# Layer-0 block attention: queries and outputs by seven block products, softmax sums on ScalarE, one PSUM bank for each kind of result

## The chip, the cores and the metric

The kernel runs on one core of a Trainium2 chip. The metric is the device time of one launch in microseconds (us); for one core that is the time of the core itself. A time is the median of several runs. Everything is computed in fp32.

The engines are named as in the profile: PE is TensorE (matmuls and transposes), PEld its weight loads, DVE is VectorE, ACT is ScalarE, POOL is GpSimd, SP is SyncE, which issues most DMAs. A matmul takes a stationary operand (its "weights", here mostly 128x128) and streams a moving operand of up to 512 columns through it. An fp32 matmul shows as two records in the trace. Results land in PSUM, which has eight banks of 128 x 512 fp32.

## The reference, cut to what matters

A decoder of two layers over x of shape (8, 112, 512), which is 896 tokens. Each layer has self-attention, cross-attention to a context, and a feed-forward part. The feed-forward part of layer 0 is itself a block: attention with 32 query heads and 4 key/value heads of dimension 128, and then a mixture of 32 experts. The change is in that inner attention:

```python
h = _rmsnorm(hidden_states, ln1_w)             # (8, 112, 512)
q = (h @ Wq).reshape(B, S, 32, 128)            # Wq: 512 x 4096
k = (h @ Wk).reshape(B, S, 4, 128)
v = (h @ Wv).reshape(B, S, 4, 128)
q = _rope(q, pos); k = _rope(k, pos)
k = jnp.repeat(k, 8, axis=2); v = jnp.repeat(v, 8, axis=2)
scores = jnp.einsum('bqhd,bkhd->bhqk', q, k) / sqrt(128)
scores = jnp.where(causal, scores, -1e9)
attn = softmax(scores)
o = jnp.einsum('bhqk,bkhd->bqhd', attn, v).reshape(B, S, 4096) @ Wo   # Wo: 4096 x 512
x = resid + o
...
h = _rmsnorm(x, ln2_w)                         # then the router and the experts
```

## The kernel before, in words

Tokens are held in seven tiles of 128 (`x[t]`, `y[t]`), and the normalised tokens transposed as `hT`, four 128-row chunks (`KC`) of 896 columns, used in two halves of 448 (`HALF`). `y` is the residual and the sum of the block.

`l0_block_attention` first computes keys `kT`, values `v` and the queries of the first head group. Then it runs over eight head groups `hg` of four heads each, and in a group over the eight sequences `b` of 112 tokens. A head group reads one 512x512 slice of Wq (`wq`) and one of Wo (`wo`). A step (hg, b) issues:

- `probabilities`: four score matmuls (L888) into a `sc_ps` bank, then on DVE scale and mask (L893), row maximum (L898) and its subtraction (L297), on ACT one exp for four heads (L298), on DVE the sum (L901) and reciprocal (L903), on POOL the product by it (L904).
- `gather_weights`: the expert weights are copied into one DRAM tensor for the experts stage, 192 copies of 256 KB spread over the 64 steps (L931). A tiny DMA that reads a row of `s` (L929) makes these copies keep pace with the attention, since SP issues its queue in order.
- `project_queries`: one of eight query blocks of the next head group, four matmuls of 448 columns (L259), and its rope (`rope_halves`): one DVE product (L841), two half products (L844), one POOL addition (L848).
- `average` of the step two before: four transposes of the probabilities (L304), an ACT copy `pT` (L306), the product with the values (L913), an ACT copy into `oT` (L917).
- `project_out` of a token tile some five steps before (`LAG`): four matmuls of 512 columns (L259) and a DVE addition into `y` (L922).

Matmul banks (0, 1), score banks (2, 3), transpose banks (4, 5) and output banks (6, 7) go in turns of two. In this block the order on each engine is left to the tile scheduler, before and after the change: the Python order is a priority, and the scheduler moves instructions of an engine against one another. Buffers come from pools with a set number of slots, and a new tile in a slot waits for the last reader of the old one.

Layer 1's feed-forward already forms its matmuls as block products by `seven_products` (in the listing after the change it has moved up). It splits both operands in 2x2 blocks. Eight block products become seven, on sums of blocks: `row_sums` makes four sums of the stationary blocks and `column_sums` four of the moving blocks. The seven products go to banks a, b and c, where some add up in place, and some are copied by ACT (L1414) so that they can be added to more than one result. Its sums and combinations are L1387 to L1397 and L1961 to L1972, its last additions into `x` L2021.

Of the kernel before, what the change touches and what calls it, by code (L numbers as in the profile page):

```python
# [58 lines left out]
def decoder(ctx: ExitStack, tc: tile.TileContext, a, out: bass.AP):  # L59
# [756 lines left out]

    def block_norm(y, t, root):

        mvr = row_scales(x[t], root, (ONCE, twice(1e-5)))
        yield  # L820
        xn = normed_rows()
        normed(xn, x[t], mvr, mvr[:, 3:4])
        shift = sm.tile([P, 1], FP, tag="shift", name="shift", bufs=8)
        V.tensor_scalar(shift, mvr[:, 0:1], mvr[:, 2:3], -1.0, ALU.mult, ALU.mult)
        A.activation(y[t], x[t], AF.Identity, bias=shift, scale=mvr[:, 2:3])
        return xn
# [23 lines left out]
    def l0_block_attention(y, hT, late, weights, prepare):  # L850
# [5 lines left out]

        wk_, wv = load_w(a["f0_wk"], "f0_wk"), load_w(a["f0_wv"], "f0_wv")
        with phase("f0", "tile") as p0:
            kT = p0.tile([P, 4, NT], FP, tag="kT", name="kT")
# [10 lines left out]
            v = p0.tile([S, B, D], FP, tag="v", name="v")  # L870
            for half in range(2):
                for g in range(4):
                    rope_halves(kT[:, g, half * HALF : (half + 1) * HALF], project_T(hT, wk_, g, half))
                for j in range(4):
                    project_queries(qT, wq, 4 * half + j)
                if half == 0:
                    for xn, t in late:
                        transpose_tile(hT, xn, t, ln1w)
            for b in range(B):
                pp = mm_ps()  # L880
                matmul_k(pp[:S, :], lambda k: hT[:, k, b * S : (b + 1) * S], lambda k: wv[:, k, :])
                A.copy(v[:, b, :], pp[:S, :])

            def probabilities(hg, qT, b):
                sc = sc_ps()
                tok = slice(b * S, (b + 1) * S)
                for j in range(4):
                    T.matmul(  # L888
                        sc[:S, j * S : (j + 1) * S], qT[:, j, tok], kT[:, hg // 2, tok],
                        start=True, stop=True,  # L890
                    )
                s = work[0].tile([S, 4, S], FP, tag="s", name="s", bufs=4)
                V.scalar_tensor_tensor(  # L893
                    s, sc[:S, : 4 * S].rearrange("p (j q) -> p j q", j=4),
                    128.0**-0.5, causal4, ALU.mult, ALU.add,
                )
                mx = sm.tile([S, 4], FP, tag="mx", name="mx")
                V.tensor_reduce(mx, s, AX.X, ALU.max)  # L898
                softmax_exp(s, mx)
                den = sm.tile([S, 4], FP, tag="den", name="den")  # L900
                V.tensor_reduce(den, s, AX.X, ALU.add)  # L901
                rec = sm.tile([S, 4], FP, tag="rec", name="rec")
                V.reciprocal(rec, den)  # L903
                G.tensor_tensor(s, s, rec.unsqueeze(2).to_broadcast([S, 4, S]), ALU.mult)  # L904
                return s

            outs = o_ps()

            def average(hg, oT, b, s):
                pT = transpose_probs(s, "pT")  # L910
                po = outs[b % 2]
                kv = hg // 2
                T.matmul(  # L913
                    po[:, : 4 * S], v[:, b, kv * P : (kv + 1) * P],
                    pT.rearrange("p j q -> p (j q)"), start=True, stop=True,
                )
                A.copy(  # L917
                    oT[:, :, b * S : (b + 1) * S], po[:, : 4 * S].rearrange("p (j q) -> p j q", j=4)
                )

            def project_out(oT, wo, t):
                V.tensor_tensor(y[t], y[t], project_rows(oT, wo, t), ALU.add)  # L922

            halves = [a[n].rearrange("e p k n -> (e p) (k n)") for n in ("e0_wg", "e0_wu", "e0_wd")]

            def gather_weights(step, s):
# [3 lines left out]
                for i, src in enumerate(halves):  # L930
                    nc.sync.dma_start(weights[r, i * KC * NI : (i + 1) * KC * NI], src[r, :])  # L931

            waiting, finished = [], []
            for hg in range(8):
# [4 lines left out]
                else:  # L939
                    prepare()  # L940
                for b in range(B):
                    waiting.append((hg, oT, b, probabilities(hg, qT, b)))
                    gather_weights(hg * B + b, waiting[-1][3])
                    if hg < 7:
                        project_queries(qT_next, wq, b)
                    if len(waiting) > 2:
                        average(*waiting.pop(0))

                    if b < NTT:
                        finished.append((oT, wo, b))  # L950
                    if len(finished) > LAG:
                        project_out(*finished.pop(0))
                qT = qT_next
            for one in waiting:
                average(*one)
            for one in finished:
                project_out(*one)
# [424 lines left out]


    def row_sums(dst, top, bottom, eng):


        eng.tensor_tensor(dst(0), bottom[0], bottom[1], ALU.add)  # L1387
        eng.tensor_tensor(dst(1), dst(0), top[0], ALU.subtract)
        eng.tensor_tensor(dst(2), top[0], bottom[0], ALU.subtract)
        eng.tensor_tensor(dst(3), top[1], dst(1), ALU.subtract)  # L1390

    def column_sums(dst, left, right, eng):

        eng.tensor_tensor(dst(0), right[0], left[0], ALU.subtract)  # L1394
        eng.tensor_tensor(dst(1), right[1], dst(0), ALU.subtract)
        eng.tensor_tensor(dst(2), right[1], right[0], ALU.subtract)
        eng.tensor_tensor(dst(3), left[1], dst(1), ALU.subtract)  # L1397

    def seven_products(banks, n, terms, top, bottom, rows, left, right, columns, copies, take):

        a, b, c = (bank[:, :n] for bank in banks)

        def product(dst, lhs, rhs, first=False, part=None):
            for k in range(terms) if part is None else part:
                T.matmul(dst, lhs(k), rhs(k), start=first and k == 0, stop=k == terms - 1,  # L1410
                         skip_group_check=True)

        def copied(i):
            A.copy(copies[i], a)  # L1414
            return copies[i]

        few = range(terms if terms < 4 else terms // 2)
        product(a, top[0], left[0], first=True)
        m1 = copied(0)
        yield  # L1420
        product(c, rows[0], columns[0], first=True)
        product(a, rows[1], columns[1])
        u2 = copied(1)
        product(b, top[1], left[1], first=True, part=few)
        product(a, rows[2], columns[2])
        u3 = copied(2)
        yield
        take(1, 1, c, u3)
        product(b, top[1], left[1], part=range(len(few), terms))
        take(0, 0, b, m1)  # L1430
        product(a, bottom[1], columns[3])
        take(1, 0, a, None)
        product(c, rows[3], right[1])
        take(0, 1, c, u2)

    def in_turn(products):

        last = iter(())
        for one in products:
            next(one)  # L1440
            all_of(last)
            next(one)
            last = one
        all_of(last)
# [471 lines left out]
    def l1_feed_forward():  # L1916


        with phase("f1") as p0:
# [4 lines left out]
            def of_hT(k, half):  # L1924
                return lambda kk: hT[:, 2 * k + kk, half * HALF : (half + 1) * HALF]

            def of(block):
                return lambda kk: block[:, kk, :]

            with ExitStack() as pools:  # L1930
                gp = pools.enter_context(tc.tile_pool(name="gates", bufs=1))
                tokens = [gp.tile([P, 2, HALF], FP, tag=f"tok{i}", name=f"tok{i}") for i in range(4)]
                for kk in range(2):
                    column_sums(lambda i: tokens[i][:, kk, :],
                                *([of_hT(k, half)(kk) for k in range(2)] for half in range(2)), V)

                def projected(w, p, banks, take):

                    def block(m, k):
                        c = (2 * p + m) * P  # L1940
                        return w[:, 2 * k : 2 * k + 2, c : c + P]

                    sums = gp.tile([P, 4, 2, P], FP, tag="sums", name="sums", bufs=3)
                    row_sums(lambda i: sums[:, i], *([block(m, k) for k in range(2)] for m in range(2)),
                             G)
# [3 lines left out]
                        banks, HALF, 2, *([of(block(m, k)) for k in range(2)] for m in range(2)),  # L1949
                        [of(sums[:, i]) for i in range(4)],  # L1950
                        *([of_hT(k, half) for k in range(2)] for half in range(2)),
                        [of(t) for t in tokens], copies, take,
# [196 lines left out]
```

## Time and profile before

| | |
|---|---|
| median of 3 runs | 2036.39 us (2034.69 to 2037.57) |
| the profiled execution | 2040.25 us |
| its span, first to last instruction | 2038.4 us |
| mean granted TensorE clock | 0.976 of full speed |
| PE busy | 1930.7 us, 95% of the span |
| DVE, ACT, POOL busy | 956.7, 589.5, 723.2 us |
| DMA | 209.65 MB, 103 GB/s on average |

The profile is one execution. Busy times are shares of the whole span, an average over stages with different limits, so the stage that is changed is read by itself: in the stretch from 406.7 to 897.8 us the attention loop runs. Lines with a line number (L259) belong to the source line, and where a helper such as `matmul_k` issues the work of several callers, they are told apart by the names of the operands. `f_wq` is a query weight slice, `f_wo` an output one. A group's row reads: line, engine, operation, output<-inputs, shapes, count, then busy us and the mean duration in ns, then the idle time of the engine before it and what ended it. A row of the timeline reads: start, length, engine, line, operation, and how many records are put together in it. A row of a tile has the shortest, median and longest duration in ns and the first and last start.

### The profile page before, as it was taken

To read this page: it belongs to the slowest core of one execution; us is meant where nothing else is said; L and a number is where in the kernel's file an instruction comes from. 1 tells how busy PE (TensorE), PEld (TensorE's weight loads), DVE (VectorE), ACT (ScalarE), POOL (GpSimd) and SP (SyncE) were. 2 spreads that over 40 slices of the span, in tenths; PEclk is the share of its full clock that TensorE was granted. 3 is DMA by queue.
4 is the path that set the end of the run, shared out by engine and by line. 5 is a ranking of instruction groups with operands and counts; after the bars stand their busy time and mean duration, and the time that the engine had idled before them with its cause. 6 is when DMAs were issued, how large, how long until landed. Compare 5 with 4: busy or idle time off the path is not lost. (4 is left out here: it accounts for less than half of the span.)

```text
span 2038.4 us, 26870 instructions
## 1 busy us (share of the span) xinstructions
PE 1930.7 (95%) x10113; PEld 1187.9 (58%) x10113; DVE 956.7 (47%) x1983; ACT 589.5 (29%) x1373; POOL 723.2 (35%) x875
## 2 busy tenths in 40 slices
PE   8999998999999999998999999989889898899999
PEld 4545664455555555554778888864555544445568
DVE  4662556375666656645222222214686556522260
ACT  3543321121122212232111111112466636422200
POOL 2253041132222222221456666631354302344371
PEclk9999989999999999989999999999999999999999
DMA  4105010143344343544886776754001120211100
GB/s 177 42 22 173 13 42 32 57 134 129 126 138 138 131 129 104 161 180 156 268 235 128 214 160 152 187 100 125 22 22 34 54 60 22 84 42 42 41 6 31
DMA packets 82024, 209.65 MB, mean 103 GB/s; under 512 B 32979, under 2 KB 38227, under 8 KB 72788
## 3 DMA queue, kind: packets, MB, share of 16 engines
q1 hardware_dynamic: 57588, 134.27, 20.0%
q0 software_dynamic: 24288, 73.47, 14.2%
q8 instruction: 86, 1.41, 0.3%
q14 instruction: 62, 0.51, 0.1%
HBM read 245.31 MB, written 78.76 MB: 159 GB/s over the span
## 5 line engine op out<-in xcount | busy, mean ns | idle before, releaser
L259 PE MATMUL bank<-f_wo,oT 128*128 128x512 f32 x448 | 210.5, 594 | 0.0
L259 PE MATMUL bank<-hT,f_wq 128*128 128x448 f32 x512 | 202.6, 540 | 0.0
L80 PEld LDWEIGHTS bank<-hbT,wb 128*128 128x128 f32 x1408 | 164.2, 192 | 20.6 <-issue 20.6
L904 POOL TENSOR_TENSOR s<-s,rec 112x448 f32<-112x448 f32 x64 | 59.8, 934 | 322.1 <-ACT pT L306 252.2
L80 DVE TENSOR_TENSOR hidb<-sgb,bank 128x256 f32<-128x256 f32 x66 | 27.8, 422 | 291.1 <-ACT sgb L80 229.4
L80 PE MATMUL bank<-hbT,wb 128*128 128x128 f32 x1408 | 164.3, 275 | 0.0
L259 PEld LDWEIGHTS bank<-hT,f_wq 128*128 128x128 f32 x512 | 93.8, 190 | 78.2 <-issue 77.8
L80 POOL TENSOR_TENSOR st<-st,rec 112x448 f32<-112x448 f32 (+1 forms) x95 | 82.9, 904 | 147.7 <-DVE rec L80 83.4
L259 PEld LDWEIGHTS bank<-f_wo,oT 128*128 128x128 f32 x448 | 80.7, 190 | 76.0 <-issue 76.0
L80 POOL DMA_INDIRECT acc<-ob,row_out x66 | 106.3, 1611 | 35.0 <-issue 18.3
L80 ACT ACTIVATE st<-st,mxs 112x112 f32<-112x112 f32 (+1 forms) x383 | 111.0, 379 | 0.0
L298 ACT ACTIVATE s<-s 112x448 f32<-112x448 f32 x64 | 36.9, 577 | 244.0 <-DVE s L297 234.3
L922 DVE TENSOR_TENSOR y<-y,bank 128x512 f32<-128x512 f32 x56 | 38.5, 688 | 124.6 <-PE bank L259 124.6
L848 POOL TENSOR_TENSOR qT<-qT,qs 128x448 f32<-128x448 f32 x64 | 72.4, 1132 | 63.3 <-DVE qs L844 63.3
L844 DVE TENSOR_TENSOR qs<-bank,shape_consts 64x448 f32<-64x448 f32 x144 | 89.5, 622 | 2.9
L80 PE MATMUL bank<-wb,hidb 128*128 128x512 f32 x176 | 84.5, 603 | 0.0
L80 ACT ACTIVATE sgb<-bank 128x256 f32<-128x256 f32 x66 | 25.4, 384 | 202.6 <-PE bank L80 179.0
L80 POOL DMA_INDIRECT hrow<-hrows,row_in x66 | 63.9, 969 | 47.0 <-DVE free L80 23.2
L80 POOL DMA_INDIRECT wb<-weights,wrow x44 | 46.3, 1052 | 95.9 <-PE bank L80 74.1
L1410 PE MATMUL bank<-tok,sums 128*128 128x448 f32 x192 | 78.1, 541 | 2.0 <-DVE tok L1394 1.4
L80 ACT ACTIVATE ob<-bank,pw 128x512 f32<-128x512 f32 x66 | 45.4, 688 | 118.8 <-PE bank L80 117.3
L888 PEld LDWEIGHTS bank<-kT,qT 128*112 128x112 f32 x512 | 59.6, 178 | 27.6 <-issue 25.6
(407 smaller groups left out, 3680.9 us busy)
## 6 DMA issues: line engine op xcount, KB each, us to landing
weights<-in_e_wg SPq DMA_DIRECT2D x64, 256.0 KB
weights<-in_e_wu SPq DMA_DIRECT2D x64, 256.0 KB
weights<-in_e_wd SPq DMA_DIRECT2D x64, 256.0 KB
f_wq<-in_f_wq SPq DMA_DIRECT2D x8, 1024.0 KB
f_wo<-in_f_wo SPq DMA_DIRECT2D x8, 1024.0 KB
cTe<-in_ctxT SPq DMA_DIRECT2D x8, 558.0 KB
f_wg<-in_f_wg SPq DMA_DIRECT2D x4, 1024.0 KB
f_wu<-in_f_wu SPq DMA_DIRECT2D x4, 1024.0 KB
```

The source lines that it names most:

```text
L80: done = issue(*args, **kw)
L259: T.matmul(dst, lhs(k), rhs(k), start=(k == 0), stop=(k == n - 1))
L298: A.activation(s, s, AF.Exp)
L844: V.tensor_tensor(qs[lo : lo + 64], src[hi : hi + 64], sin0[lo : lo + 64].unsqueeze(1).to_broadcast([64, HB, S]), ALU.mult,)
L848: G.tensor_tensor(d, d, qs, ALU.add)
L888: T.matmul(sc[:S, j * S : (j + 1) * S], qT[:, j, tok], kT[:, hg // 2, tok], start=True, stop=True,)
L904: G.tensor_tensor(s, s, rec.unsqueeze(2).to_broadcast([S, 4, S]), ALU.mult)
L922: V.tensor_tensor(y[t], y[t], project_rows(oT, wo, t), ALU.add)
L1410: T.matmul(dst, lhs(k), rhs(k), start=first and k == 0, stop=k == terms - 1, skip_group_check=True)
```

## The change: seven products, exps with sums, single banks, and fills

`seven_products` becomes a generator with a stop after almost every product, so that its pieces can be laid between the steps of the softmax. What it does in the block attention:

1. Queries of head groups 1 to 7 are formed by `query_products`: two calls a group, each for two heads and both halves of the tokens. Their row sums of `wq` are made on POOL, the token sums once on DVE. The token sums need room; they lie in the tiles of `x`, which are saved in DRAM (`far_x`) ahead of the loop and loaded back after it.
2. Outputs of all head groups are formed by `output_products` for three pairs of token tiles, in half widths of 256 columns; the seventh tile as before (`last_output`). Row sums of `oT` on POOL, column sums of `wo` on DVE. `take` adds a copy into `y` on POOL and then a bank into `y` on DVE.
3. Keys and values of the key/value groups 2 and 3 wait in DRAM (`far_k`, `far_v`) until head group 2 and 4.
4. The softmax takes the minimum of negated scores; four exps, one for each head, each with its own bias and with the sum as `accum_out`, replace subtraction, exp and sum. The product by the reciprocal goes out one step later.
5. The tiny DMA that sets the pace reads `s` after the scaling, ahead of the exps, of which the one of head 0 overwrites what it reads.
6. Scores use bank 5, transposes bank 6, averages bank 7, and the product banks are 4 and, in turns, (0, 1) and (2, 3).
7. The pieces lie in a list `fills`. Three times a step `fill` issues pieces up to a share of their costs (QUERY 150, OUTPUT 86), and ropes of finished queries come from the list `later`.

The diff, cut to its core:

```diff
+    def row_sums(dst, top, bottom, eng):
+        eng.tensor_tensor(dst(0), bottom[0], bottom[1], ALU.add)
+        eng.tensor_tensor(dst(1), dst(0), top[0], ALU.subtract)
+        eng.tensor_tensor(dst(2), top[0], bottom[0], ALU.subtract)
+        eng.tensor_tensor(dst(3), top[1], dst(1), ALU.subtract)
...
+    def seven_products(banks, n, terms, top, bottom, rows, left, right, columns, copies, take):
+        a, b, c = (bank[:, :n] for bank in banks)
...
+        product(a, top[0], left[0], first=True)
+        m1 = copied(0)
+        yield
+        product(c, rows[0], columns[0], first=True)
+        yield
+        product(a, rows[1], columns[1])
+        u2 = copied(1)
+        yield
+        few = range(terms if terms < 4 else terms // 2)
+        product(b, top[1], left[1], first=True, part=few)
+        if terms < 4:
+            take(0, 0, b, m1)
+        yield
+        product(a, rows[2], columns[2])
+        u3 = copied(2)
+        yield
+        take(1, 1, c, u3)
...
+        product(a, bottom[1], columns[3])
+        take(1, 0, a, None)
+        yield
+        product(c, rows[3], right[1])
+        take(0, 1, c, u2)
...
+            for t in range(NTT):
+                nc.sync.dma_start(far_x[t * P : (t + 1) * P, :], x[t])
...
+            def query_products(qT, wq, p):
+                top, bottom = blocks_of(wq, p)
+                sums = p0.tile([P, 4, 2, P], FP, tag="qsum", name="qsum", bufs=2)
+                row_sums(lambda i: sums[:, i], top, bottom, G)
+                yield
+                copies = [normed_rows()[:, :HALF] for _ in range(3)]
+                def take(m, half, pp, more):
+                    if more is not None:
+                        d = more if m == half == 1 else pp
+                        V.tensor_tensor(d, pp, more, ALU.add)
+                        pp = d
+                    later.append((qT[:, 2 * p + m, half * HALF : (half + 1) * HALF], pp))
...
+            def output_products(oT, wo, columns, p):
...
+                row_sums(lambda i: sums[:, i], top, bottom, G)
+                yield
+                copies = [p0.tile([P, NI], FP, tag=f"oc{i}", name="oc", bufs=1) for i in range(3)]
+                def take(m, n, pp, more):
+                    d = y[2 * p + m][:, n * NI : (n + 1) * NI]
+                    if more is not None:
+                        G.tensor_tensor(d, d, more, ALU.add)
+                    V.tensor_tensor(d, d, pp, ALU.add)
...
-                V.tensor_reduce(mx, s, AX.X, ALU.max)
-                softmax_exp(s, mx)
-                V.tensor_reduce(den, s, AX.X, ALU.add)
+                V.tensor_reduce(mn, s, AX.X, ALU.min)
...
+                for j in range(4):
+                    A.activation(s[:, j, :], s[:, j, :], AF.Exp, bias=mn[:, j : j + 1], scale=-1.0,
+                                 accum_out=den[:, j : j + 1])
...
+            def fill(upto):
+                while fills and spent[0] < upto and fills[0][0] in ready:
+                    pieces, cost, _ = fills[0]
+                    try:
+                        next(pieces)
+                        spent[0] += cost
+                    except StopIteration:
+                        fills.pop(0)
+                        make_ready()
+                if later:
+                    rope_halves(*later.pop(0))
...
+                for b in range(B):
...
+                    scores(hg, qT, b)
+                    fill(base + each * (3 * b + 1))
+                    s, mn = find_minima()
+                    waiting.append((hg, oT, b, s))
+                    gather_weights(hg * B + b, s)
+                    if undivided:
+                        divide(*undivided.pop())
+                    one = waiting.pop(0) if len(waiting) > 2 else None
+                    if one:
+                        pT = turned(one[3])
+                    fill(base + each * (3 * b + 2))
+                    if one:
+                        average(*one[:3], pT)
+                        averaged[0] += 1
+                        make_ready()
+                    if b == 4:
+                        columns = output_sums(wo)
+                    if b == 5:
+                        add(output_products(oT, wo, columns, 0), OUTPUT, done + 3)
+                    undivided.append(exps(s, mn))
+                    fill(base + each * (3 * b + 3))
...
+            for t in range(NTT):
+                nc.sync.dma_start(x[t], far_x[t * P : (t + 1) * P, :])
```

In a head group the fills come in this order: the outputs of the former group's tiles 2 and 3, the first query pair of the next group, the former group's tiles 4 and 5 and its tile 6, the second query pair, and the group's own tiles 0 and 1. The copies of a product are made by ACT (L847 after the change), a score step's minimum is L1087, an exp L1093, the additions into `y` L1050 on POOL and L1051 on DVE. `l1_feed_forward` uses the same helpers.

## The prediction

> **What bounds the kernel now.** I read the busy row of the page first, then the busy times by stretch, then the waits of TensorE in the changed stretch, then its timeline.
>
> ```profile
> PE 1930.7 (95%) x10113; PEld 1187.9 (58%) x10113; DVE 956.7 (47%) x1983; ACT 589.5 (29%) x1373; POOL 723.2 (35%) x875
> ...
> 406.74:897.80 491.06, 489.61 (x1780) 261.95 (x1779) 303.25 (x547) 115.84 (x215) 125.96 (x122) 1.00 0.41 136
> 1900.00:2038.00 138.00, 134.45 (x497) 93.86 (x495) 43.46 (x47) 14.94 (x31) 54.44 (x39) 1.00 0.06 22
> ...
> PE bank L913 <- ACT pT L306: 0.9, 1, 0.9
> PE bank L304 <- POOL s L904: 0.6, 2, 0.3
> ```
>
> The second and third lines are stretches: length, then busy time (and rows) of PE, weight loads, DVE, ACT, POOL, then granted clock, DMA share, GB/s. The attention loop (406.7 to 897.8 us) is bound by TensorE alone: 489.6 of 491.1 us, clock 1.00, and in all of it TensorE waits for another engine 1.5 us (the two wait lines: total, times, longest). So work taken off PE is gained in full, as long as no wait takes its place. The third line is the layer-1 feed-forward, which already uses the seven products: 3.5 us idle in 138.
>
> One step of the loop, from TensorE's timeline:
>
> ```profile
> 605.25 0.95 PE L888 MATMUL bank<-kT,qT 128*112 128x112 f32 x8
> 606.04 3.19 PE L259 MATMUL bank<-hT,f_wq 128*128 128x448 f32 x8
> 609.06 0.55 PE L304 MATMUL bank<-ident,s 112*112 112x112 f32 x4
> 609.45 1.04 PE L259 MATMUL bank<-f_wo,oT 128*128 128x512 f32 x2
> 610.32 0.99 PE L913 MATMUL bank<-pT,v 112*128 112x448 f32 x2
> 611.14 2.74 PE L259 MATMUL bank<-f_wo,oT 128*128 128x512 f32 x6
> 613.72 0.95 PE L888 MATMUL bank<-kT,qT 128*112 128x112 f32 x8
> ```
>
> Durations overlap, so starts count. A matmul is two records. From start to start: scores 0.79, a query block 3.02 (four matmuls of 0.758), transposes 0.39, p·v 0.76 to 0.82, an output tile 3.44 (four of 0.86). The step is 613.72 - 605.25 = 8.47 us; seven such and one without output (5.02) make a head group of 64.3 us.
>
> The other engines' prices:
>
> ```profile
> L904 POOL TENSOR_TENSOR s<-s,rec 112x448 f32<-112x448 f32 x64 | 59.8, 934 | 322.1 <-ACT pT L306 252.2
> L848 POOL TENSOR_TENSOR qT<-qT,qs 128x448 f32<-128x448 f32 x64 | 72.4, 1132 | 63.3 <-DVE qs L844 63.3
> L2021 POOL TENSOR_TENSOR x<-x,ucopy 128x256 f32<-128x256 f32 x9 | 6.9, 775 | 31.4 <-ACT ucopy L1414 31.4
> 1886.61 0.73 POOL L1387 TENSOR_TENSOR sums<-f_wg 128x256 f32<-128x256 f32 x1 [2.08 <-PE bank L1410]
> 1887.30 0.73 POOL L1389 TENSOR_TENSOR sums<-f_wg 128x256 f32<-128x256 f32 x1
> L965 ACT ACTIVATION_READ_ACCUMULATOR bank<-y x7: 186/187/193, 872.3 to 899.3; 128x1 f32 x7
> L1394 DVE TENSOR_TENSOR colsum<-f_wd x4: 680/684/691, 1937.7 to 1940.1; 128x512 f32<-128x512 f32 x4
> L1397 DVE TENSOR_TENSOR colsum<-f_wd,colsum x4: 2828/2834/2839, 1952.2 to 1971.5; 128x512 f32<-128x512 f32 x4
> 2001.48 5.34 PE L1410 MATMUL bank<-f_wd,hid 128*128 128x256 f32 x24
> 2006.66 3.62 PE L1410 MATMUL bank<-colsum,hid 128*128 128x256 f32 x16
> ```
>
> A row sum on POOL comes every 0.69 us. An accumulating exp leaves a second record of 187 ns. A column sum on DVE takes 0.68 alone and 2.83 beside POOL's row sums. 24 half-width records take 5.18 us, 0.216 each, against 0.430 at 512 columns: half the width costs half.
>
> **The change, part by part.**
>
> *PE work removed.* Queries of groups 1 to 7: 28 matmuls of 448 columns for 32, so 7 x 4 x 0.758 = 21.2 us. Outputs: before 28 x 0.86 = 24.1 a group; after, three pairs of tiles by seven products (42 half-width matmuls of 0.43) and tile 6 as before (4 x 0.86): 21.6. Saved 2.5 x 8 = 20.0. Together 41.2 us, 2%. Here a rule speaks against the change: the Trainium skill, Perfetto Trace Analysis, section Matmuls, calls larger matmuls more efficient. By the 0.216 against 0.430 above nothing is lost; I take the trace.
>
> *One bank a kind.* The same section wants independent groups to rotate through PSUM banks. Scores now have bank 5 alone. Before, DVE starts on the scores 0.2 us after the last one and takes 0.62 (L893). If every step's scores had to wait for that, the rule would make it 64 x 0.83 = 53 us, and the forecast some 2105. But the next scores come a step (7 us or more) later, so by the trace this costs 0, and so do single banks for transposes and p·v. I take 0. Where the pairs (0,1) and (2,3) are re-used inside one product, the margin is thin: a's first result must be copied (0.25 to start, 0.37, 0.09 back: 0.71, from the ACT rows of 128x256) during c's two half-width matmuls (0.87). 0.16 us of slack, if ACT is free.
>
> *Added to ACT.* Four exps a step. One of 112x112 repeats at 0.29 to 0.38 in this kernel; with the 0.187 record I take 0.52, bounds 0.29 and 0.57. A step: 2.08 for 0.58 before. Copies: 9 x 0.37 and 6 x 0.53 a group. Sum 8 x (2.08 + 1.06) + 6.5 = 32 us of 60: covered on average. But a burst of three exps (1.56) in front of a product's copy eats the 0.16.
>
> *DVE.* L297 and the sum L901 go (1.3 us a step); six query additions, twelve additions into y (0.42 by a 128x256 row) and four column sums come: about 38 to 44 us of 60 a group. Column sums: 2.15 extra each where they fall beside POOL's sums, at most 8 a group. In the order that the scheduler leaves they mostly stand apart; I take 0, upper 1.6 of exposed time.
>
> *POOL.* Before 2.0 us a step. Now a group has 8 x (0.93 + 1.09), 20 row sums of 0.69 and 9 additions of 0.70: 36 to 39 us of 60. Again enough on average, but they bunch.
>
> *The softmax chain.* From the scores to the product by the reciprocal it is 0.2 + 0.62 + 0.66 + 2.1 + 0.17 + 0.93, some 5 us with latencies. The divide goes out one step later and the transposes stay two steps behind the scores, some 15 us: hidden by two steps of TensorE work, unless the bursts below eat them. 0.
>
> *Stalls.* I followed the built order of instructions of a middle group (4), each with the duration above, engine by engine. PE idles where:
> 1. First output product of the group: the third copy stands behind exps and the oT copy, 0.6; the c product waits for POOL's addition, then DVE's, 0.45; p·v behind exps, 0.35. Sum 1.4.
> 2. The group's own first pair of tiles. The first copy stands behind three exps, whose minimum is late because DVE is in the rope: 1.8. Then POOL: from the end of the rope products it has, back to back, three rope additions (3.3), eight row sums (5.5: four for the next queries, four for the next outputs), one softmax product (0.93) and three additions into y (2.1), 11.8 us. Only the last of these frees DVE's addition and so bank 3, another 0.6. PE has 7.4 us of work there and the 1.8 of waiting: short by 12.4 - 9.2 = 3.2; with a later start of POOL's bunch (an ACT copy) 3.7. 5.5 in all.
> 3. Third product, 0.4; and weight loads no longer hidden after some four stalls, 0.19 each, 0.7.
>
> 8.0 us a group, 48 for six. Group 0 has no outputs of a former group, 2; group 7 no queries beside its outputs, 1.2 on each of three products, some 4; the two last products have nothing beside them, 2.2 each, 4.5. Sum 58.5.
>
> *DMA.* SP issues seven stores and seven loads of x (256 KB), the far keys and values: about 7 MB at a DMA share of 0.41. The tiny copy of s (L929) now waits for the scaled scores, not the divide. SP needs 0.69 to issue it and about 1.0 to land; ACT's last exp (head 0) waits for that. Minimum and three exps take 0.66 + 1.56 = 2.2, so it is hidden; bounds 0 and rival B. The keys and values of groups 2 and 3 are asked for at step 3 of head groups 2 and 4, thirteen steps ahead of their first use. The loads of x go out at the end of the loop; their first use (L1040) comes after the norms and transposes of seven tiles. 0; upper 3 for the values' stores behind weight loads. The layer-1 feed-forward keeps its PE order: 0 to 2 either way.
>
> *Sum.* -41.2 - 1.5 (old waits) + 58.5 = +15.8 on the profiled execution's 2040.25 = 2056. It lies 3.9 above the median; the same difference gives 2052. Stalls cannot be negative, so the gain is at most 42.7. The work removed pays for stalls of about 5.4 us a group (41.2 + 1.5 - 10.5 = 32.2, by six).
>
> **Rivals.**
> A, faster: POOL's bunch at bank 3 is harmless. The mechanism: items of the bunch run earlier (in the group's slack) or shorter, so bank 3 is free when PE arrives. For it: POOL is 60% busy, and layer 1 runs these products with 3.5 us idle in 138. Against it: no softmax runs there, and the order of POOL's queue is fixed. It decides where the 11.8 fall under about 8.6 (7.4, the first waits, less the way back). Then item 2 goes, 5.5 x 6 = 33: 2019; with all stalls gone 1996.
> B, slower: ACT's last exp waits for the tiny copy in every step, and the bank copies queue behind it. For it: SP has 2.4 us of issuing a step, and "weights<-s" was waited for 48 times before, up to 2.3 us. Against it: that wait was on SP alone. It decides where issue and landing exceed 2.2; at 0.6 a step, 64 x 0.6 = 38: 2090.
> C, nothing done: that seven products don't come to fewer matmuls. The built kernel has 28 for 32 and 46 (42 half) for 28, so no.
>
> **How the numbers follow.** Forecast case (6 to 11 us a group): 0.62, its own range 2041 to 2072. A: 0.27, 1996 to 2032. B: 0.11, 2078 to 2100. A difference of 0.2%, 4 us, is about what can be told from none. The forecast's low edge gives 0.06 to "same". Range 2014 to 2080: it leaves out A with nearly all saved and most of B. Faster 0.26, same 0.06, slower 0.68.
>
> **What would show it.** Right: PE in the block busy about 41 us less, a loop of about the same length or longer, and in the waits of PE new lines of a few us each a group, of bank against DVE's addition into y (L1051) and ACT's copies (L847), POOL solid before the longest. The row of an exp with its record near 0.52. Wrong: PE waits under 4 us a group (A), or ACT exps waiting for "weights<-s" (B), or column sums at 2.8.

## The result and the profile after

The changed kernel takes 2058.87 us (median of 4 runs, 2054.07 to 2061.70) against 2035.54 us before (4 runs, with those shown above): a ratio of 1.0112, 95% interval 1.0089 to 1.0135. It is slower by 23.3 us. The forecast was 2052, from a sum of +15.8. The profiled execution took 2061.70 us, its span is 2060.0. One execution in the experiments below, of the kernel with matmuls added in the stall, took 4765.98 us and is left out of its median.

First the busy times of the engines over the span, then the busy times by stretch (length, busy of PE, weight loads, DVE, ACT, POOL, granted clock, DMA share, GB/s): the attention loop, one head group, and the five microseconds behind the longest wait of that group.

```profile
PE 1916.5 (93%) x10345; PEld 1242.7 (60%) x10345; DVE 946.5 (46%) x1993; ACT 687.5 (33%) x1939; POOL 890.8 (43%) x1099
...
406.94:921.80 514.86, 470.27 (x2017) 315.91 (x2015) 284.26 (x539) 213.07 (x764) 284.99 (x337) 0.96 0.41 138
...
656.58:661.55 4.97, 4.97 (x16) 4.30 (x17) 1.98 (x5) 0.00 (x0) 0.57 (x1) 0.51 0.00 0
...
640.00:708.10 68.10, 62.06 (x263) 41.53 (x261) 38.37 (x72) 26.37 (x96) 38.21 (x45) 0.95 0.42 138
```

The loop has grown from 491.1 to 514.9 us although TensorE is busy 19.3 us less in it. The stretches ahead of and behind it changed by +0.2 and -2.4 us, so the whole loss is here. The clock of the loop is 0.96 for 1.00 before. A group takes 68.1 us instead of 64.3.

Who TensorE waited for in the loop (total, times, longest):

```profile
PE bank L843 <- DVE y L1051: 28.4, 14, 4.8
PE bank L843 <- ACT oc L847: 8.6, 11, 1.2
PE bank L1104 <- POOL s L1100: 6.5, 6, 3.3
PE bank L1111 <- ACT pT L1106: 0.2, 1, 0.2
```

That is 43.7 us in place of 1.5. The account of the loop: -41.2 for matmuls removed; +43.1 for idle time, which is 44.6 us (514.86 - 470.27) for 1.5 before; and +14.6 for seven stretches at a lower clock, where the starts of the matmuls lie 1.4 to 2.4 us further apart in sum than at full clock. This makes +16.5. Most of the other 7 of the +23.8 are restarts: in each of 42 gaps, three before, the next matmul starts some 0.16 us later than the idle time alone explains, 6.4 us in all. Two differences that nearly cancel are left out: p·v is 4 us shorter in all, and other matmuls together some 5 us longer. As an example of a restart, in the lines below, from 649.38 to 651.49 it is 2.11 us, for 0.76 of matmuls and 1.19 of waiting.

The place where it is lost, TensorE's timeline (start, length, ..., wait ahead and its releaser):

```profile
649.38 0.92 PE L1111 MATMUL bank<-pT,v 112*128 112x448 f32 x2
651.49 1.13 PE L843 MATMUL bank<-osum,oT 128*128 128x256 f32 x4 [1.19 <-ACT oc L847]
656.58 2.08 PE L843 MATMUL bank<-f_wo,osums 128*128 128x256 f32 x4 [3.96 <-DVE y L1051]
658.45 1.70 PE L1076 MATMUL bank<-kT,qT 128*112 128x112 f32 x8
659.94 1.78 PE L843 MATMUL bank<-f_wo,oT 128*128 128x256 f32 x4
661.55 1.89 PE L843 MATMUL bank<-osum,osums 128*128 128x256 f32 x8
663.28 0.55 PE L1104 MATMUL bank<-ident,s 112*112 112x112 f32 x4
```

This is the group's own first pair of output tiles. It waits 1.19 us for a copy on ACT and 3.96 us for the addition into `y`. The matmuls behind the longer wait then take about twice their time: scores, 0.79 us from start to start elsewhere, take 1.49 here (658.45 to 659.94). The second stretch row above gives the clock there, 0.51. Meanwhile POOL:

```profile
644.22 1.14 POOL L932 TENSOR_TENSOR qT<-qT,qs 128x448 f32<-128x448 f32 x1 [2.37 <-DVE qs L928]
645.32 0.73 POOL L820 TENSOR_TENSOR qsum<-f_wq 128x256 f32<-128x256 f32 x1
...
648.18 0.73 POOL L820 TENSOR_TENSOR osums<-oT 128x256 f32<-128x256 f32 x1
...
653.77 0.73 POOL L1050 TENSOR_TENSOR y<-y,oc 128x256 f32<-128x256 f32 x1
654.45 0.95 POOL L1100 TENSOR_TENSOR s<-s,rec 112x448 f32<-112x448 f32 x1
655.34 0.73 POOL L1050 TENSOR_TENSOR y<-y,oc 128x256 f32<-128x256 f32 x1
656.10 0.75 DVE L1051 TENSOR_TENSOR y<-y,bank 128x256 f32<-128x256 f32 x2 [4.69 <-POOL y L1050]
```

POOL works without a gap from 644.22 to 656.07, 11.85 us, and the last addition of this row of work is the one that DVE (last line), and then TensorE, are waiting for. POOL is busy only 38.2 of the group's 68.1 us: its load is not the bound, its queue at this point is.

### The profile page after: what moved, and what is told of

Same layout as the page of the kernel before. It is cut to its first block, busy times and chain, and to the rows that moved or that the text cites. A ratio compares the mean times of both kernels' runs of the same rounds, so it can differ in the third digit from the quotient of the medians.

```text
span 2060.0 us, 28199 instructions
## 1 busy us (share of the span) xinstructions
PE 1916.5 (93%) x10345; PEld 1242.7 (60%) x10345; DVE 946.5 (46%) x1993; ACT 687.5 (33%) x1939; POOL 890.8 (43%) x1099
## 4 chain that ended last, share of the span: by engine, by line
PE 32%; POOL 7%; issue 6%; DVE 5%; DMA 4%; ACT 2%; SPq 1%; POOLq 0%; DVEq 0%; ACTq 0%
PE bank L80 15%; PE bank L843 12%; PE bank L259 3%; POOL acc L80 3%; DMA acc<-ob,row_out 2%; POOL hrow L80 2%; DVE mxs L80 1%; SPq L791 1%; DMA hrow<-hrows,row_in 1%; POOL st L80 1%; DVE den L80 1%; ACT st L80 1%; POOL wb L80 1%; PE bank L1709 0%; ACT pTt L80 0%
## 5 line engine op out<-in xcount | busy, mean ns | idle before, releaser
L1093 ACT ACTIVATE s<-s,mn 112x112 f32<-112x112 f32 x256 | 97.2, 381 | 78.7 <-DVE mn L1087 68.2
L1051 DVE TENSOR_TENSOR y<-y,bank 128x256 f32<-128x256 f32 x96 | 38.9, 416 | 116.9 <-POOL y L1050 80.5
L1076 PEld LDWEIGHTS bank<-kT,qT 128*112 128x112 f32 x512 | 65.5, 190 | 16.2 <-issue 11.8
L1050 POOL TENSOR_TENSOR y<-y,oc 128x256 f32<-128x256 f32 x72 | 52.8, 734 | 49.1 <-ACT oc L847 49.0
L928 DVE TENSOR_TENSOR qs<-bank,shape_consts 64x448 f32<-64x448 f32 x116 | 72.1, 621 | 1.7
L843 PE MATMUL bank<-osum,osums 128*128 128x256 f32 x288 | 72.1, 380 | 0.0
L1076 PE MATMUL bank<-kT,qT 128*112 128x112 f32 x512 | 66.2, 274 | 0.0
L80 PE MATMUL bank<-ident,st 112*112 112x112 f32 (+1 forms) x384 | 51.2, 266 | 14.6 <-POOL st L80 10.9
```

The source lines that it names most:

```text
L80: done = issue(*args, **kw)
L928: V.tensor_tensor(qs[lo : lo + 64], src[hi : hi + 64], sin0[lo : lo + 64].unsqueeze(1).to_broadcast([64, HB, S]), ALU.mult,)
L1050: G.tensor_tensor(d, d, more, ALU.add)
L1051: V.tensor_tensor(d, d, pp, ALU.add)
L1076: T.matmul(bank[5][:S, j * S : (j + 1) * S], qT[:, j, tok], keys[hg // 2 % 2][:, tok], start=True, stop=True)
L1093: A.activation(s[:, j, :], s[:, j, :], AF.Exp, bias=mn[:, j : j + 1], scale=-1.0, accum_out=den[:, j : j + 1])
```

## The experiments

Times are medians; "group" is the period of a middle head group, read from TensorE's timeline (the same piece of work in two successive groups), which carries far less noise than the whole time. The ratios on record are not the quotients of these medians and differ from them by up to 0.002. The last line of the table is the changed kernel.

| kernel | us | ratio to before (95%) | group, us |
|---|---|---|---|
| before | 2035 to 2037 | 1 | 64.3 |
| query row sums on DVE | 2048.49 | 1.0064 (1.0041 to 1.0087) | 64.7 |
| additions into y on DVE | 2017.97 | 0.9915 (0.9889 to 0.9941) | 61.7 |
| matmuls added in the stall | 2052.72 | 1.0105 (1.0071 to 1.0140) | 65.8 |
| program order | 2055.76 | 1.0102 (1.0079 to 1.0124) | 64.5 |
| additions on DVE, old softmax | 2035.71 | 0.9989 (0.9976 to 1.0001) | 63.2 |
| additions on DVE, program order | 2053.10 | 1.0070 (1.0044 to 1.0097) | 65.1 |
| seven products for queries only | 2016.09 | 0.9894 (0.9868 to 0.9920) | 60.9 |
| seven products for outputs only | 2030.09 | 0.9952 (0.9933 to 0.9970) | 62.5 |
| first output pair as before | 2021.96 | 0.9923 (0.9892 to 0.9955) | 61.7 |
| the same, additions on DVE | 2013.62 | 0.9887 (0.9853 to 0.9921) | 61.0 |
| the change | 2058.87 | 1.0112 (1.0089 to 1.0135) | 68.1 |

The theory that these were to test: the additions into `y` stand in POOL's queue behind row sums and ropes, and this holds bank c; the waiting is then paid a second time by a halved clock. The rivals: ACT's bursts or DVE's load are the cause, and POOL only happens to come last; or the output products stall by themselves.

**Additions into y on DVE.** One word in `take` of `output_products`:

```diff
-                        G.tensor_tensor(d, d, more, ALU.add)
+                        V.tensor_tensor(d, d, more, ALU.add)
```

> The additions of copies into y (L1050) are made by DVE instead of POOL. Theory (POOL's bunch holds bank 3): bank c no longer waits for anything in POOL's queue, so the wait of 3.96 us and the half-speed stretch (2.35) go in six groups: 38 us less, about 2021. Rival (DVE is the next bound: nine more additions of two SBUF operands, which may take turns with POOL's): half of it comes back as waits for DVE, about 2040; if these additions take the time of POOL's instructions beside them, 2059 or more.

2017.97 us. The order on TensorE is the same but for a few rows. The waits in its loop (total, times, longest):

```profile
PE bank L843 <- ACT oc L847: 10.2, 11, 1.4
PE bank L1104 <- POOL s L1100: 6.2, 5, 3.3
PE bank L843 <- DVE y L1051: 2.2, 6, 0.4
```

The 28.4 us for DVE's `y` have become 2.2, no half-speed stretch is left in the middle groups (one is, in group 0), and the group falls by 6.4 us (forecast 3.96 + 2.35 = 6.3). These additions cost DVE more than the 0.34 us that half of a 128x512 row would give: 411 to 1176 ns, but DVE has the room, 44.5 us busy of 61.7. POOL still has its bunch of ropes and row sums, without a gap from 626.94 to 637.31 us, and it now does no harm. So it is the place of these nine small additions in POOL's queue that made the change slower.

**Query row sums on DVE.** `row_sums(..., G)` becomes `row_sums(..., V)` in `query_products`; the order on TensorE is unchanged.

> The row sums of the query weights are made by DVE instead of POOL; TensorE's order is the same. Theory (POOL's bunch holds bank 3): four of the sums, 2.75 us, leave the bunch in front of the addition into y; the wait of bank 3 falls from 3.96 to about 1.2 us, and the half-speed stretch after it goes (2.35): (2.75 + 2.35) x 6 = 31 us less, about 2028, less what eight sums of some 0.35 cost DVE. Rival (ACT's bursts and the late minimum are the cause, POOL only comes last): the wait stays within 1 us, and DVE, busier by 3 us a group, makes it 2059 or more.

2048.49 us, group 64.7: 3.4 us less where 5.1 was forecast. The wait for `y` falls from 3.96 to 2.07 (less than the 2.75 taken out), the copy's from 1.19 to 0.75, the clock stays at 1.00, but a new wait of 0.97 for `pT` and its restart come up. This holds for three groups, from 632 to 830 us. In the two before them the waits are 1.37 and 2.07 us, and one of 3.84 for a copy on ACT, with a lowered clock behind each, so that the whole kernel gains 10 us and not the 31 of the theory. So POOL's bunch is the cause of the wait in this experiment too; emptying it in part pays in part. That DVE's row sums delay the softmax, and so `pT`, fits the new wait but was not tested.

**Matmuls added in the stall.** In `seven_products`, for the first output pair only:

```diff
         take(1, 0, a, None)
         yield
+        for _ in range(idle):                    # idle = 4
+            product(b, bottom[1], right[1], first=True)
         product(c, rows[3], right[1])
```

> Work is added: ahead of the last product of the first output pair of each group, eight matmuls of 256 columns into bank 4 that nobody reads (3.46 us where TensorE runs at full speed). Theory (a stall of about 4 us is paid twice, once as waiting and once as a stretch at half clock): they fill the wait of 3.96 us, the clock stays at 1.00, and 2.35 us a group are saved in about six groups: 12 to 14 us less, about 2046. Rival (the half clock has another cause than the stall): the same as without them, 2059; and where TensorE was not waiting for another engine in this place, 3.5 x 8 = 28 us more.

TensorE's timeline of the same place, and the stretch behind it one group earlier:

```profile
647.51 1.13 PE L843 MATMUL bank<-osum,oT 128*128 128x256 f32 x4 [1.21 <-ACT oc L847]
648.48 3.62 PE L843 MATMUL bank<-f_wo,oT 128*128 128x256 f32 x16
652.61 1.13 PE L843 MATMUL bank<-f_wo,osums 128*128 128x256 f32 x4 [0.52 <-DVE y L1053]
653.58 0.95 PE L1078 MATMUL bank<-kT,qT 128*112 128x112 f32 x8
...
586.82:591.80 4.98, 4.98 (x30) 4.47 (x31) 2.03 (x5) 1.97 (x9) 1.66 (x2) 1.00 0.00 0
```

The third row still waits for `y`, at the same distance from the first (5.10 us against 5.09), but the added work fills all but half a microsecond of it. The clock is now 1.00, and the scores take 0.79 us again. The group is 65.8 us: 2.3 less than the change for 3.5 us more of matmuls. Over the whole kernel that is hardly to be told: 2049.18, 2052.72 and 2059.67 us, against 2054.07 to 2061.70 for the change; the forecast was 2046. In group 0 the wait for `y` was only 1.76 us, and with the added work a wait of 2.26 for POOL's product stands in its place. What is shown is the price of the halved clock in a group, not a faster kernel.

**Program order.** The loop over head groups is wrapped in `with in_order():`.

> The loop over head groups keeps the program's order on TensorE, DVE, ACT and POOL instead of the scheduler's. Theory (the stalls come of the order of POOL's and ACT's queues, not of their load, which is 38 and 26 us of 68): with row sums and exps where the program puts them, between the pieces, most waits go: 2000 to 2025. Rival (the load in the place is the bound, whatever the order): the waits of bank 3 and of the first copy stay, 2050 to 2070.

2055.76 us, a miss: the time is in the rival's range, but the waits are not the rival's. The group falls to 64.5, the wait for `y` to 0.7 and 0.4, but a wait of 2.57 for a copy on ACT takes over, with 0.6 and 0.2 at other copies. The order was indeed what made the long wait; the program's own order makes others. Groups 2 to 6 gain 10 us in all, and the ends lose as much: from the first scores to the end of group 1 it takes 119.9 us instead of 115.6, and the last group 71.3 instead of 65.9. With the additions on DVE as well:

> The additions of copies into y on DVE, and the loop in program order. Theory (additions on POOL cost the pinned order its waits for DVE's y, 0.7 and 0.4 us a group, as well as some for copies): 2050 falls by 7 x 1.5 to about 2045; it stays above the scheduler's 2018, since the long wait there, 2.6 us, is for a copy on ACT. Rival (the same queue of POOL stands behind that copy): the 2.6 goes too, 2020 to 2030.

2053.10 us and a group of 65.1. The wait for the copy is still 2.59, one of the two waits for `y` goes and the other falls to 0.3, but more of the groups lose clock behind the 2.59. So moving the additions is worth 41 us in the scheduler's order and 3 in this one. The theory's 2045 was missed by 8; its point, that the long wait of this order is not for POOL's additions, stands. What delays the copy on ACT was not followed.

**The softmax as before, additions on DVE.** `find_minima` and `exps` go back to maximum, subtraction on DVE, one exp and a sum on DVE:

```diff
-                for j in range(4):
-                    A.activation(s[:, j, :], s[:, j, :], AF.Exp, bias=mn[:, j : j + 1], scale=-1.0,
-                                 accum_out=den[:, j : j + 1])
+                softmax_exp(s, mx)
+                V.tensor_reduce(den, s, AX.X, ALU.add)
```

> The additions of copies into y on DVE (as in the kernel of that name) and the softmax as before the change: maximum, subtraction on DVE, one exp of four heads on ACT, sum on DVE. Theory (what is left, 1.4 and 0.7 us a group in front of the copies on ACT, are bursts of exps): these waits fall below 0.3 and it gains up to 2 us a group, 2003 to 2010. Rival (DVE, which goes from 44.5 to about 55 us of a group's 62, is late with everything): bank waits for DVE appear, 2025 to 2050.

2035.71 us, 18 us slower than with the sums on ACT, as the rival had it: waits of 1.62 and 0.66 us a group for DVE's `y` appear, and one of 1.29 for a copy on ACT remains. Bursts of exps are not the whole reason for that last one; and the part of the change that moves the softmax from DVE to ACT is worth its price.

**Seven products for one half.** For the queries alone, outputs tile by tile:

> Seven products for the queries alone; the outputs are formed tile by tile in 512 columns as before, everything else as in the changed kernel. Theory (the long stall belongs to the additions into y behind POOL's bunch, which go here): a group takes 64.3 - 3.0 = 61.3 us and a waiting of at most 1, group 0 and the end some 7 in all: 2020 to 2026. Rival (the queries' copies, ropes and row sums stall TensorE by themselves): a group of 64 us or more, 2036 or more.

2016.09 us, faster than the theory's 2020 to 2026; the whole of the saving arrives. Two groups of its loop:

```profile
550.65:672.48 121.83, 121.83 (x450) 66.97 (x449) 69.42 (x122) 47.76 (x172) 44.53 (x48) 1.00 0.45 146
```

TensorE is never idle in them. For the outputs alone, in two first versions:

> Seven products for the outputs alone; the queries are formed block by block from eight products as before, everything else as in the changed kernel. Theory (POOL's bunch): the row sums of the query weights go from the bunch (2.75 us), the wait of bank 3 falls from 3.96 to about 1.2 and its half-speed stretch goes: a group of 64.3 - 2.5 + 3.5 = 65.3 us, about 2044. Rival (the output products stall whatever else is in POOL's queue): the wait of bank 3 stays near 4 us, 68 us or more a group, 2060 or more.

> Seven products for the outputs alone; the queries are formed block by block from eight products, each with its rope at once, everything else as in the changed kernel. Theory (the bunch on POOL needs both halves of the change: without the row sums of the query weights and the three ropes at a time it is short): waits of bank 3 under 1 us, no half-speed stretch, a group of 64.3 - 2.5 + 1 = 62.8 us, about 2022 to 2030. Rival (the output products stall whatever else is in POOL's queue): the wait of bank 3 stays near 4 us, 67 us or more a group, 2055 or more.

In both, the sums of tokens, which then served nothing, still replaced a part of `hT` that the plain queries read; in the first, ropes could also read a bank that was already in use again. So the queries differ, other tokens can go to the experts, and the totals (2073.97 and 2077.55) say nothing on the change. With the sums of tokens left out:

> Seven products for the outputs alone, and the sums of tokens, which nothing needs then, left out; the queries block by block from eight products, each with its rope at once; everything else as in the changed kernel. Theory (the bunch on POOL needs both halves of the change): waits of bank 3 under 1 us, no half-speed stretch, a group of about 62.5 us: 2036 - 7 x 1.8 = 2023, 2018 to 2030. Rival (the output products stall whatever else is in POOL's queue): the wait of bank 3 near 4 us, 2055 or more.

2030.09 us, group 62.5, at the upper edge of the theory's range; the waits of bank 3 in the middle groups are 0.7 at most:

```profile
605.73:668.23 62.50, 62.24 (x269) 41.53 (x268) 34.95 (x65) 23.84 (x89) 31.82 (x37) 1.00 0.45 150
```

It gains 6.5 rather than 13 us; the first and last groups keep waits of 0.2 to 2.7 us in ten places. Each half of the change alone makes the kernel faster; together they make it slower. The account that fits both runs: each half's work on POOL is done in time, and in the one place where three ropes, eight row sums and three additions meet, it is not.

**The first output pair as before.** Only tiles 0 and 1 of the group, which fall beside the ropes, are formed tile by tile; then the same with the additions on DVE:

```diff
-                        add(output_products(oT, wo, columns, 0), OUTPUT, done + 3)
+                        add(plain_outputs(oT, wo, (0, 1)), OUTPUT, done + 3)
```

> Both halves of the change, but the pair of output tiles that falls beside the ropes (tiles 0 and 1 of the group itself) is formed tile by tile as before. Theory (only that pair meets POOL's bunch): the waits of 1.19 and 3.96 us and the half-speed stretch go, the pair costs 0.83 us more matmul time; a group of 68.1 - 7.5 + 0.8 = 61.4 us or a little less, 2008 to 2020. Rival (the bunch only moves to the next pair's additions): a wait of over 2 us elsewhere in the group, 2030 or more.

> As the kernel before it in this list, with the additions of copies into y on DVE. Theory: nothing of the path is left on POOL; what remains is up to 0.7 us a group in front of copies on ACT: 60.5 us a group, 2005 to 2013. Rival (DVE's additions, slow beside POOL's, are now in the way): no faster than without, 2010 to 2022.

2021.96 and 2013.62 us, groups of 61.7 and 61.0. The first is 0.3 us a group, and in all 2 us, above the range that the theory gave; the second is 0.5 a group and in all 0.6 us above its range. The long wait is gone. These runs alone would not say why, since the pair's four row sums and three additions leave POOL together with its products; the additions moved by themselves do. The last kernel beats both the kernel before (0.9887, 0.9853 to 0.9921) and the change; from the queries alone and from the additions on DVE it cannot be told apart, as the intervals overlap.

## Why the prediction was right, point by point

- **Matmul work, -41.2 us.** Confirmed: the queries alone bring the group from 64.3 to 60.9 (forecast 61.3), and the half-width matmuls have their forecast price (eight records from 661.55 to 663.28, 0.216 each). The 0.4 us more come mostly from p·v, which nobody forecast: 0.82 us from start to start before, 0.76 after (665.41 to 666.17), eight times a group.
- **The long stall, 5.5 us a group.** Measured 1.19 + 3.96 = 5.15, in the product, the bank and behind the queue that were named; POOL's bunch 11.85 for a forecast of 11.8. Groups 1 and 2 waited 5.5 and 5.6, group 6 3.25. Rival A, in which this bunch does no harm, is excluded for the change as it stands. The kernel that takes the additions out of the queue is at 2018, where A had 2019, but that closeness is in part luck: A took 33 us off 2052, and the run took 41 off 2058.87, lowered clock included. (With all stalls gone A's sums give 1994, not 1996.)
- **The restart, 0.7 us a group.** This is the term that was mis-sized. The forecast counted only weight loads that no longer hide, 0.19 us a stall, and these came out (0.16 a gap). It put the clock at nothing: after the long wait TensorE ran at 0.51 of its clock for 5 us, 2.35 us more, and seven such stretches cost the loop 14.6 us, twice the 7 that the 2052 lacks. The trace before had no wait of this length in the loop, but it had one behind it: at 987.23 us, after 4.85 us of waiting for a DMA, the clock is 0.56 over 5 us. The Trainium skill, TensorE: Matmul & The Clock Gate, section What's actually happening, has a clock of one half after an idle window of about 3.4 us that runs free; by it, with the 2.35 us measured here, the forecast would have been higher by about 6 x 2.35 = 14, some 2066, as an estimate. The rows agree on the half clock and on its dependence on where the wait falls. On the length they don't, since shorter waits lowered the clock too: one of 3.34 us in the kernel with the additions on DVE (the same wait cost nothing in the change), and one of 2.07 us, with 1.37 us of waiting and four records shortly ahead of it, in the kernel with the query row sums on DVE.
- **First product (1.4) and third (0.4).** Smaller: 0.59 + 0.17 and nothing in the middle groups. An exp with its sum repeats at 0.385 us, not 0.52: the bursts are shorter. The group's sum was 8.0; measured is 68.1 - 58.4 = 9.7, where 58.4 is the 60.9 of the queries alone less 2.5 for the outputs. The error of the whole is smaller than the clock that was left out, because these two products were put 1 us a group too high and p·v became shorter. That is luck.
- **Group 0 and the end.** 2 and 8.5 were forecast. Group 0 waits 7.2 us (0.27 + 1.41 + 3.34 + 1.76 + 0.40), mostly for POOL's product by the reciprocal, which the forecast had at nothing; group 7 and the end wait 2.8. The sum is about right, the places are not: luck again.
- **Column sums** took 1.2 us each in the median, not 0.68; next to nothing in TensorE's waits points to them (0.4 us).
- **Single banks.** Costed at 0, right: no wait of TensorE in the loop is for the scores' bank.
- **Rival B, the tiny DMA.** ACT waited for it 0.3 us in the whole loop: no effect.

## What to carry to other kernels

Work that is taken off the bounding engine brings small steps to the others, and what counts is not their sum but what stands in front of the step that frees a bank: follow that step's queue, one instruction at a time, at the place where pieces of several kinds meet. A short step that a bank waits for does not belong into the queue of long work that nobody waits for; moving nine additions of 0.7 us a group to another engine turned 23 us of loss into 17 of gain. And a wait of some microseconds on TensorE can be paid one and a half times: here 3.96 us idle and then 2.35 at half clock. Look for such a place anywhere in the trace before, also outside of the stage that is changed.

## What was not expected of the hardware

- The granted clock after a wait, in the change: 0.50 to 0.58 over the next five microseconds after waits of 3.96 to 4.79 us, five of five; 0.69 after 2.60 (with 0.65 a little ahead of it). The same wait of 3.34 us in group 0, between the same matmuls, was followed by 1.00 in the change (first row) and by 0.66 with the additions on DVE (second row). The third row is the kernel before, after the 4.85 us at 987.23.

```profile
437.80:443.00 5.20, 5.19 (x28) 3.62 (x29) 3.59 (x7) 2.57 (x10) 4.01 (x5) 1.00 0.01 2
438.09:443.09 5.00, 5.00 (x15) 2.69 (x16) 2.12 (x4) 2.19 (x8) 2.37 (x3) 0.66 0.00 0
987.23:992.23 5.00, 5.00 (x14) 2.93 (x15) 0.69 (x1) 0.46 (x1) 0.22 (x1) 0.56 0.72 177
```

- In the kernel in program order the same wait of about 2.57 us was followed by 0.70 in one group and by 1.00 in two others. With the query row sums on DVE the clock halved only 1.3 us after the end of a wait of 3.84 (1.13 us for the first four half-width records, 2.07 for the next).
- The second record of an accumulating exp hides almost wholly: exp and record start at 642.44, 642.74, and the next exp at 642.83, so 0.39 us an exp with its sum, where lengths of 0.38 and 0.19 had been read as a sum.
- An addition on DVE of two operands in SBUF (128x256) took 411 to 1176 ns, with a median of 427. All 34 of 440 ns or more ran beside an instruction of POOL, but so did ten of the 38 shorter ones.
